# Attention heads of two sequences planned as couples: ten query blocks in five groups of scores, values placed beside a later group

## The chip, the core and the metric

The kernel runs on one core of one Trainium2 chip. Its engines are TensorE (PE; its weight loads are listed apart as PEld), VectorE (DVE), ScalarE (ACT), GpSimd (POOL) and SyncE (SP), which issues the DMAs. The metric is device time in microseconds (us) of one execution, the median of several runs. Every engine works its own list of instructions in order and waits on semaphores for the others.

## The reference, cut to what matters

```python
# x: (8, 512, 1024) float32; 16 heads of 64; everything in float32
def attention(h):                    # h = layernorm(x)
    q, k, v = h @ Wq, h @ Wk, h @ Wv           # split into 16 heads
    q, k = rotary(q), rotary(k)
    logits = einsum("bhqd,bhkd->bhqk", q, k)   # causal: -1e9 above the diagonal
    attn = softmax(logits / 8)
    return einsum("bhqk,bhkd->bhqd", attn, v) @ Wo
x = x + layernorm(attention(layernorm(x)))
x = x + layernorm(layernorm(x) @ W.T + bias + lora)
```

## The kernel before, in words

All large products are made by a two-level fast scheme: a product is cut into 7 x 7 = 49 small ones. One small product is a *tick*. Work that goes beside the products is planned by hand: `at(tick, fn, kind)` puts a function on a tick, and `run(tick, filler)` (L177) issues a tick in this order: first every event of kind `"pe"` (work for PE), in the order in which the events were planned; then the tick's small product with its drain (`filler`); then the plain events and the `"post"` events, again in the order of planning. Nothing reorders the instructions afterwards: this is each engine's list.

The kernel has four parts. First the values V of all eight sequences are computed and stored (`vd`). Then the QK loop makes queries and keys and runs the attention beside them. Then come the output projection and the feed-forward product, with the norms beside them.

The QK loop has `UQ` = 8 *stages* (`u`, L995 to L1010) of 49 ticks. A stage makes Q and K of eight heads for two sequences. `unit_product` (L953) issues its tick: four matmuls of 128x256, which the trace lists as eight records (L636), then the drain of the product before (L113 to L129: one or two copies or sums of 512 columns out of PSUM, on DVE or ACT), then the load of the slot eight ticks ahead (L608 to L622: 2 x 256 KB; the ring has nine slots). `plan_unit` (L691) puts the combining sums (L654) and the rotary embedding (`rotate`, L660 to L690) into a stage, mostly from tick 33 on to tick 14 of the next stage; the four rotations of a stage work on DVE and POOL with instructions of 1024 columns and end in DMAs (L687), eight for each, that spread Q and K into the tile `qk`. As `cq` has one buffer of each tag, a later drain into `A_q`, `B_q`, `D_q`, `E_q` or `F_q` must wait until the DMAs that read the tile have landed.

The attention of stage `u` - 1 runs in stage `u`. Its unit is a *pair*: two heads (j = 0, 1; 64 partitions each) of one sequence. A stage has `PAIRS` = 8 of them: four head tiles `i`, each for two sequences `s`. A pair has four query blocks of 128 rows; by causality block `qb` needs (qb + 1) x 128 key columns. The methods of `Pair` are:

- `load` (L735): the values of the pair, one DMA of 256 KB (pool `v`, three buffers).
- `scores` (L739): two matmuls per query block, one for each head, into a PSUM tile `s` of [128, 2, 512] floats, of which there is one buffer. The heads use partitions 0 to 63 and 64 to 127 of the operands.
- `exps` (L757): per block and head one DVE instruction (scale, mask, row minimum; L768) and one ACT exponential with its sum (L778), into a tile `pr` (four buffers).
- `scale` (L783): per block a reciprocal on DVE (L786) and two multiplications on ACT (L792).
- `transpose` (L794) and `keep` (L810): 128x128 transposes on PE into two PSUM tiles `tp` (two buffers) and copies into `pT`, by ACT for head 0 and by DVE for head 1.
- `values` (L823) and `store` (L835): eight matmuls of 512 to 128 columns with 64 output partitions per head, then one copy by DVE.
- `sum` (L847): four subtractions on POOL and two DMAs, for the last head tile only.

`Pair.plan` (L860) puts a pair on the ticks from `base`: scores of the groups (0, 1), (2,) and (3,) on +0, +2, +4 (384, 384 and 512 columns a head), their scaling on +4, +6, +8, their transposes on +6, +8, +10 (6, 6 and 8 blocks for the two heads), the values on +12. In stages 1 to 6 the pairs start 6 or 7 ticks apart (L1000 to L1002). So the values of one pair, the transposes of the next and the scores of the one after mostly fall on one tick. Stage 7 carries the pairs of stage 6 five ticks apart, and those of stage 7 follow behind with little beside them.

Of the kernel before, what the change touches and what calls it, by code (L numbers as in the profile page):

```python
# [10 lines left out]
F32 = mybir.dt.float32  # L11
I32 = mybir.dt.int32
AF = mybir.ActivationFunctionType
ALU = mybir.AluOpType
# [118 lines left out]
def sandwich_kernel(  # L133
# [587 lines left out]

    ops = {}

    class Pair:


        def __init__(self, u, n):
            self.u = u
            self.i, self.s = divmod(n, 2)
            self.g, bp = divmod(u, B // 2)  # L730
            self.b = 2 * bp + self.s
            self.name = f"{u}_{n}"
            self.pr, self.sm, self.ps = {}, {}, {}

        def load(self):  # L735
            self.v = work2["v"].tile([P, NT, P], F32, tag="v", name=f"v_{self.name}")
            nc.sync.dma_start(out=self.v, in_=vd[self.b][:, :, ts(NH * self.g + self.i, P)])

        def scores(self, qbs):  # L739
            qT, kT = (qk[self.u, self.i][:, :, self.s, w] for w in range(2))  # L740
            ps = ps_s.tile([P, 2, S], F32, tag="s", name=f"s_{self.name}_{qbs[0]}")
            at = 0
            for qb in qbs:
                L = (qb + 1) * P
                for j in range(2):
                    r = slice(j * HD, (j + 1) * HD)
                    nc.tensor.matmul(  # L747
                        ps[:, j, at : at + L],
                        lhsT=qT[r, qb],
                        rhs=kT[r, : qb + 1],  # L750
                        start=True,
                        stop=True,
                    )
                self.ps[qb] = ps[:, :, at : at + L]
                at += L

        def exps(self, qbs):  # L757
            pr = work2["work"].tile([P, 2, S], F32, tag="pr", bufs=4, name=f"pr_{self.name}_{qbs[0]}")
            at = 0
            for qb in qbs:  # L760
                L = (qb + 1) * P
                v = self.pr[qb] = pr[:, :, at : at + L]
                at += L
                nm = work2["small"].tile([P, 2], F32, tag="nm", name=f"nm_{self.name}_{qb}")
                sm = self.sm[qb] = work2["small"].tile([P, 2], F32, tag="sm", name=f"sm_{self.name}_{qb}")
                for j in range(2):

                    nc.vector.tensor_tensor_reduce(  # L768
                        out=v[:, j, :],
                        in0=self.ps[qb][:, j, :],  # L770
                        in1=work2["mask"][:, S - L :],
                        scale=-1.0 / HD**0.5,
                        scalar=3.0e38,
                        op0=ALU.add,
                        op1=ALU.min,
                        accum_out=nm[:, j : j + 1],
                    )
                    nc.scalar.activation(  # L778
                        v[:, j, :], v[:, j, :], AF.Exp,
                        bias=nm[:, j : j + 1], scale=-1.0, accum_out=sm[:, j : j + 1],  # L780
                    )

        def scale(self, qbs):  # L783
            for qb in qbs:
# [7 lines left out]
                        nc.scalar.mul(v, v, rs[:, j : j + 1])  # L792

        def transpose(self, qbs):  # L794
            if qbs[0] == 0:
                self.pT = [
                    work2["work"].tile([P, NT, S], F32, tag="pT", name=f"pT_{self.name}_{j}")
                    for j in range(2)
                ]
            self.pt = []  # L800
            for j in range(2):
                pt = ps_t.tile([P, NT, P], F32, tag="tp", name=f"ptp_{self.name}_{qbs[0]}_{j}")
                n = 0
                for qb in qbs:
                    for kb in range(qb + 1):
                        nc.tensor.transpose(pt[:, n, :], self.pr[qb][:, j, ts(kb, P)], ident)  # L806
                        n += 1
                self.pt.append(pt)

        def keep(self, qbs):  # L810
            for j in range(2):

                n = self.u * PAIRS + 2 * self.i + self.s - (UQ - 1) * PAIRS
                act = -2 <= n < 1 or j == 0 and (n < 0 or qbs[0] != 2)
                copy = nc.scalar.copy if act else nc.vector.tensor_copy
                if qbs[0] == 0:
                    copy(self.pT[j][:, 0, 0 : 2 * P], self.pt[j][:, 0:2, :])
                    copy(self.pT[j][:, 1, P : 2 * P], self.pt[j][:, 2, :])
                else:
                    (qb,) = qbs  # L820
                    copy(self.pT[j][:, : qb + 1, ts(qb, P)], self.pt[j][:, : qb + 1, :])  # L821

        def values(self):  # L823
            self.po = po = ps_v.tile([P, S], F32, tag="v", name=f"po_{self.name}")
# [35 lines left out]
        def plan(self, base, last=12, alone=False):  # L860

            A, B2, C3 = (0, 1), (2,), (3,)
            at(base - 4, self.load)
            for k, qbs in ((0, A), (2, B2), (4, C3)):
                at(base + k - alone, lambda qbs=qbs: self.scores(qbs), "pe")
                at(base + k - alone, lambda _, qbs=qbs: self.exps(qbs), "post")
            for k, qbs in ((6, A), (8, B2), (10, C3)):
                at(base + k - (4 if alone else 2), lambda qbs=qbs: self.scale(qbs))
                at(base + k, lambda qbs=qbs: self.transpose(qbs), "pe")
                at(base + k, lambda _, qbs=qbs: self.keep(qbs), "post")  # L870
            at(base + last, self.values, "pe")
            if alone:
                last += 2
                at(base + last, self.store)
            else:
                at(base + last, lambda _: self.store(), "post")
            if self.i == NH - 1:
                for m, k in enumerate((0, 0, 0, 0, 1) if alone else (1, 2, 3, 4, 6)):
                    at(base + last + k, lambda m=m: self.sum(m))

    products(-B, B, lambda q: ORDER)
    psum.close()
# [112 lines left out]
    for u in range(UQ + 1):  # L995
        base = u * N2
        if u < UQ:
            plan_unit(u, base)
        if 0 < u < UQ - 1:
            for n in range(PAIRS):  # L1000
                first = 10 if u > 1 else 12
                Pair(u - 1, n).plan(base + first + (n * (N2 + 10 - first) + PAIRS // 2) // PAIRS)  # L1002
        elif u == UQ - 1:
            for n in range(PAIRS):
                Pair(u - 1, n).plan(base + 9 + 5 * n, last=11)
            for n in range(PAIRS):
                Pair(u, n).plan(base + 51 + 6 * n, alone=True)
        if u < UQ:
            for n in range(base, base + N2):
                run(n, lambda n=n: unit_product(n))  # L1010
        else:
            run(base, lambda: cur.drain(NP))
            for k in range(base + 1, base + 10):
                run(k, None)
            streams.close()
            chunks.close()

            wop, gp, cl = (tc.alloc_tile_pool(name=name, bufs=1) for name in ("w2", "g2", "cl"))
            env["cl"] = cl
            tl = tc.alloc_tile_pool(name="tl", bufs=1)  # L1020
            for k, n in (
                (10, "R11"), (10, "L11"), (15, "R12"), (17, "R22"), (21, "L12"), (24, "R21"), (31, "L22"), (42, "S1"),
            ):
                if n in ("R11", "R12", "R21", "R22"):
                    at(base + k, lambda n=n: load_right(gp, 0, n))
                else:
                    at(base + k, lambda n=n: load_sums(wop, "wo", n, n))
            for k, n in ((21, "T1"), (26, "T2"), (32, "T4"), (44, "T3")):
                for m in range(3):
                    at(base + k + m, lambda n=n, m=m: sum_right(gp, 0, n, nc.gpsimd, slice(m, m + 1)))  # L1030
            at(base + 57, next_roles)
            for n in ("R12", "R11", "R21"):
                at(base + 57, lambda n=n: load_right(gp, 1, n))
            at(base + 52, lambda: combine(0, "c11", "c11", "A", nc.vector))
            cur, ticks = None, [*range(20, 44, 3), *range(44, 57)]
            for k in range(10, 57):
                if k in (51, 56):
                    n = {51: "S2", 56: "S4"}[k]
                    load_sums(wop2, "wo", n, n)
                if k == 49:  # L1040
                    rows_qk.close()
                    wop2 = tc.alloc_tile_pool(name="w2b", bufs=1)
                    load_sums(wop2, "wo", "S3", "S3")
                if k in ticks:
                    run(base + k, lambda n=ticks.index(k): first_product(n))
                else:
                    run(base + k, None)
            cur.drain(NP)
            run_rest()
# [311 lines left out]
```

## Time and profile before

| | |
|---|---|
| three timed runs, median (lowest to highest) | 2499.29 us (2498.07 to 2499.87) |
| profiled execution, its span | 2491.9 us |
| its time outside the span | not on the page; the median of the runs is 7.4 us above the span |
| mean granted TensorE clock | 0.988 |
| busy: PE, PEld, DVE, ACT, POOL | 2394.2, 1880.4, 1744.9, 1094.4, 1490.5 us |
| start of stages 2, 3, 4, 5, 6, 7 (first tick, in the timeline) | 657.2, 807.5, 956.1, 1105.1, 1253.8, 1402.6 us |

The page is one execution. A row of the timeline reads: start, length, engine, line of the kernel, operation, output<-inputs, shape, number of merged records, and in brackets the idle time before it with what ended it. PE's matmuls overlap in the pipeline and their ends are modelled, so the length of a row is not what it costs; the difference between its start and the start of the next row is. A window row reads: stretch, its length, then the busy time of each engine in it.

### The profile page before, as it was taken

What the parts mean: (1) busy time and instruction counts of PE and PEld (TensorE: products, weight loads), DVE (VectorE), ACT (ScalarE), POOL (GpSimd) and SP (SyncE); (2) the same over time, 40 slices, a digit from 0 to 9 for tenths busy, and PEclk for the clock granted to TensorE, in tenths of its full rate; (3) what the DMA queues carried; (4) which work ended last, traced back from release to release, by engine and by line L of the source; (5) the groups of instructions that cost most, each with busy time, mean ns of one, the idle gap of its engine ahead of it and who ended that gap; (6) DMA issues with size and microseconds to landing.
All of it is one profiled execution on the core that took longest, in us unless ns stands there. A gap on an engine that the chain in (4) does not pass through costs nothing. (4 is left out here: it accounts for less than half of the span.)

```text
span 2491.9 us, 37087 instructions
## 1 busy us (share of the span) xinstructions
PE 2394.2 (96%) x12192; PEld 1880.4 (75%) x12192; DVE 1744.9 (70%) x3849; ACT 1094.4 (44%) x2749; POOL 1490.5 (60%) x1119
## 2 busy tenths in 40 slices
PE   6999999999999999999999999899999999999997
PEld 4787887877677777777777776458888878888886
DVE  8777767475857759486775957766777777766676
ACT  3323331026555556555555565763444544222222
POOL 3878875215263454637465363426777687888885
PEclk8999999999999999999999999899999999999999
DMA  7697787999899898988989895657566676434334
GB/s 261 198 299 251 241 272 235 344 307 285 238 302 285 258 328 255 328 267 297 326 264 346 250 327 174 219 182 266 178 202 212 217 278 240 137 126 153 132 106 140
DMA packets 415665, 606.00 MB, mean 243 GB/s; under 512 B 127889, under 2 KB 243601, under 8 KB 410866
## 3 DMA queue, kind: packets, MB, share of 16 engines
q1 hardware_dynamic: 415474, 603.64, 73.9%
q8 instruction: 98, 1.61, 0.3%
q14 instruction: 93, 0.76, 0.1%
HBM read 368.65 MB, written 201.33 MB: 229 GB/s over the span
## 5 line engine op out<-in xcount | busy, mean ns | idle before, releaser
L778 ACT ACTIVATE pr<-pr,nm 128x128 f32<-128x128 f32 (+3 forms) x512 | 280.9, 550 | 169.7 <-DVE nm L768 169.6
L792 ACT ACTIVATE pr<-pr,rs 128x128 f32<-128x128 f32 (+2 forms) x500 | 245.2, 549 | 119.9 <-DVE rs L786 119.8
L768 DVE CUSTOM_DVE_ANT_0 pr<-s,mask 128x128 f32<-128x128 f32 (+3 forms) x512 | 224.1, 484 | 41.8 <-PE s L747 39.7
L636 PE MATMUL acca_q_P<-xs,ls 128*128 128x256 f32 x896 | 217.3, 385 | 0.8 <-issue 0.8
L636 PE MATMUL accc_q_P<-xs,ls 128*128 128x256 f32 x896 | 217.7, 386 | 0.0
L636 PE MATMUL accb_q_P<-xs,ls 128*128 128x256 f32 x896 | 216.3, 384 | 0.8 <-DVE u_q_P L116 0.8
L1107 POOL TENSOR_TENSOR c<-c,row 128x512 f32<-128x512 f32 x120 | 160.7, 1360 | 87.4 <-ACT c L415 80.3
L636 PEld LDWEIGHTS acca_q_P<-xs,ls 128*128 128x128 f32 x896 | 165.3, 190 | 49.9 <-issue 19.1
L636 PEld LDWEIGHTS accc_q_P<-xs,ls 128*128 128x128 f32 x896 | 165.8, 190 | 48.4 <-issue 23.2
L636 PEld LDWEIGHTS accb_q_P<-xs,ls 128*128 128x128 f32 x896 | 165.4, 190 | 44.9 <-issue 6.2
L275 POOL TENSOR_TENSOR T<-R,T 128x512 f32<-128x512 f32 (+1 forms) x96 | 174.1, 1840 | 41.4 <-DVE u_P L337 21.0
L747 PE MATMUL s<-qk 64*128 64x128 f32 (+3 forms) x1024 | 193.8, 474 | 5.1 <-DVE nm L768 4.7
L806 PE MATMUL ptp<-ident,pr 128*128 128x128 f32 x1280 | 178.7, 278 | 11.0 <-DVE nm L768 4.8
L806 PEld LDWEIGHTS ptp<-ident,pr 128*128 128x128 f32 x1280 | 147.7, 142 | 43.1 <-ACT pr L792 15.8
L827 PE MATMUL po<-pT,v 128*64 128x512 f32 (+3 forms) x1024 | 157.4, 446 | 9.7 <-ACT pT L821 9.7
L562 POOL TENSOR_TENSOR wc_g<-wc_g 128x256 f32<-128x256 f32 (+1 forms) x120 | 124.1, 1053 | 65.5 <-DMA wc_g<-in_wqk_dram 43.5
L678 POOL TENSOR_TENSOR B_q<-B_q,m 128x1024 f32<-128x1024 f32 x14 | 35.0, 2497 | 199.0 <-DVE B_q L675 199.0
L827 PEld LDWEIGHTS po<-pT,v 128*64 128x64 f32 x1024 | 72.4, 139 | 102.0 <-issue 66.5
L337 DVE TENSOR_TENSOR p_P<-accb_P,p_P 128x256 f32<-128x256 f32 x109 | 45.0, 413 | 102.4 <-PE accb_P L315 53.5
L636 PE MATMUL accd_q_P<-xs,ls 128*128 128x256 f32 x448 | 108.7, 385 | 0.0
L337 DVE TENSOR_TENSOR u_P<-accb_P,p_P 128x256 f32<-128x256 f32 x109 | 46.1, 423 | 89.1 <-ACT p_P L342 89.0
L747 PEld LDWEIGHTS s<-qk 64*128 64x128 f32 x1024 | 73.1, 187 | 46.2 <-issue 27.9
(1108 smaller groups left out, 5809.7 us busy)
## 6 DMA issues: line engine op xcount, KB each, us to landing
ls<-wqk SPq DMA_DIRECT2D x392, 256.0 KB, 4.9
xs<-xop SPq DMA_DIRECT2D x392, 256.0 KB, 5.2
R<-attn SPq DMA_DIRECT2D x32, 896.0 KB, 5.5
wqk<-wc_g SPq DMA_DIRECT2D x16, 1568.0 KB, 9.3
x<-in_x_dram SPq DMA_DIRECT2D x32, 512.0 KB, 9.5
v<-vd SPq DMA_DIRECT2D x64, 256.0 KB, 5.0
attn<-ops SPq DMA_DIRECT2D x16, 1024.0 KB, 7.8
row<-in_x_dram SPq DMA_DIRECT2D x32, 512.0 KB, 5.9
```

The lines of the kernel that those rows point to most:

```text
L275: eng.tensor_tensor(RX[q, n][:, c], RX[q, x][:, c], RX[q, y][:, c], op=ALU.subtract)
L337: add = lambda out, x, a: nc.vector.tensor_tensor(out, acc[a], x, op=ALU.add)
L562: eng.tensor_tensor(out, x, y, op=op)
L636: nc.tensor.matmul(acc[:, :, w, :], lhsT=ls[:, k, w, :], rhs=xs_[:, :, k, :], start=(first and w == 0 and k == 0), stop=True, skip_group_c ...
L678: eng.tensor_tensor(v, v, m[step - 4, q], op=ALU.add)
L747: nc.tensor.matmul(ps[:, j, at : at + L], lhsT=qT[r, qb], rhs=kT[r, : qb + 1], start=True, stop=True,)
L768: nc.vector.tensor_tensor_reduce(out=v[:, j, :], in0=self.ps[qb][:, j, :], in1=work2["mask"][:, S - L :], scale=-1.0 / HD**0.5, scalar=3.0e38,
L778: nc.scalar.activation(v[:, j, :], v[:, j, :], AF.Exp, bias=nm[:, j : j + 1], scale=-1.0, accum_out=sm[:, j : j + 1],)
L792: nc.scalar.mul(v, v, rs[:, j : j + 1])
L806: nc.tensor.transpose(pt[:, n, :], self.pr[qb][:, j, ts(kb, P)], ident)
L827: nc.tensor.matmul(po[j * HD : (j + 1) * HD, kb * P :], lhsT=self.v[:, kb, ts(j, HD)], rhs=self.pT[j][:, kb, kb * P :], start=(kb == 0), s ...
L1107: nc.gpsimd.tensor_tensor(c, c, row[q, t][:, ts(h, HALF)], op=ALU.add)
```

## The change

Two module-level helpers, `scores` and `exps`, take a list of (pair, query block), so that a group may hold blocks of two pairs. The methods of `Pair` call them. `keep` opens the tiles `pT` itself, and handles any list of blocks.

`plan_couple` is new. It plans the two sequences' pairs of one head tile, `a` and `b`, together: groups of scores a0+a2, a3, a1+b1, b0+b2, b3 (512 columns a head each) on ticks +0, +2, +5, +7, +10; transposes a(0, 2) on +6, a3 on +8, a1 on +10, b(0, 2) on +13, b1 on +14, b3 on +15 (8, 8, 4, 8, 4, 8 blocks for the two heads); the scaling of each group two ticks ahead of its transposes, except a1 and b3 (one tick) and b1 (five); the values of `a` on the start of the next couple, those of `b` five ticks later. Stages 1 to 6 plan four couples in place of eight pairs, 12 ticks apart (one step a stage is 13, in stage 1 it is 11). Stage 7 is planned as before.

```diff
+    def scores(parts):
+        p, qb = parts[0]
+        ps = ps_s.tile([P, 2, S], F32, tag="s", name=f"s_{p.name}_{qb}")
+        at = 0
+        for p, qb in parts:
+            qT, kT = (qk[p.u, p.i][:, :, p.s, w] for w in range(2))
+            L = (qb + 1) * P
+            for j in range(2):
+                r = slice(j * HD, (j + 1) * HD)
+                nc.tensor.matmul(
+                    ps[:, j, at : at + L], lhsT=qT[r, qb], rhs=kT[r, : qb + 1], start=True, stop=True
+                )
+            p.ps[qb] = ps[:, :, at : at + L]
+            at += L
+    def exps(parts):
+        p, qb = parts[0]
+        pr = work2["work"].tile([P, 2, S], F32, tag="pr", bufs=4, name=f"pr_{p.name}_{qb}")
+        at = 0
+        for p, qb in parts:
+            L = (qb + 1) * P
+            v = p.pr[qb] = pr[:, :, at : at + L]
+            at += L
...
         def scores(self, qbs):
...
+            scores([(self, qb) for qb in qbs])
         def exps(self, qbs):
...
+            exps([(self, qb) for qb in qbs])
...
         def transpose(self, qbs):
-            if qbs[0] == 0:
-                self.pT = [
-                    work2["work"].tile([P, NT, S], F32, tag="pT", name=f"pT_{self.name}_{j}")
-                    for j in range(2)
-                ]
...
         def keep(self, qbs):
+            if not self.pT:
+                self.pT = [
+                    work2["work"].tile([P, NT, S], F32, tag="pT", name=f"pT_{self.name}_{j}")
+                    for j in range(2)
+                ]
...
-                if qbs[0] == 0:
+                if qbs == (0, 1):
                     copy(self.pT[j][:, 0, 0 : 2 * P], self.pt[j][:, 0:2, :])
                     copy(self.pT[j][:, 1, P : 2 * P], self.pt[j][:, 2, :])
                 else:
-                    (qb,) = qbs
-                    copy(self.pT[j][:, : qb + 1, ts(qb, P)], self.pt[j][:, : qb + 1, :])
+                    n = 0
+                    for qb in qbs:
+                        copy(self.pT[j][:, : qb + 1, ts(qb, P)], self.pt[j][:, n : n + qb + 1, :])
+                        n += qb + 1
...
+    def plan_couple(u, i, base, after):
+        a, b = (Pair(u, 2 * i + s) for s in range(2))
+        for p in (a, b):
+            at(base - 4 + 5 * p.s, p.load)
+        for k, parts in (
+            (0, [(a, 0), (a, 2)]), (2, [(a, 3)]), (5, [(a, 1), (b, 1)]), (7, [(b, 0), (b, 2)]), (10, [(b, 3)]),
+        ):
+            at(base + k, lambda parts=parts: scores(parts), "pe")
+            at(base + k, lambda _, parts=parts: exps(parts), "post")
+        for k, m, p, qbs in (
+            (6, 4, a, (0, 2)), (8, 6, a, (3,)), (10, 9, a, (1,)),
+            (13, 11, b, (0, 2)), (14, 9, b, (1,)), (15, 14, b, (3,)),
+        ):
+            at(base + m, lambda p=p, qbs=qbs: p.scale(qbs))
+            at(base + k, lambda p=p, qbs=qbs: p.transpose(qbs), "pe")
+            at(base + k, lambda _, p=p, qbs=qbs: p.keep(qbs), "post")
+        for p, k in ((a, after), (b, after + 5)):
+            at(k, p.values, "pe")
+            at(k, lambda _, p=p: p.store(), "post")
+            if i == NH - 1:
+                for m, n in enumerate((1, 2, 3, 4, 6)):
+                    at(k + n, lambda p=p, m=m: p.sum(m))
...
         if 0 < u < UQ - 1:
-            for n in range(PAIRS):
-                first = 10 if u > 1 else 12
-                Pair(u - 1, n).plan(base + first + (n * (N2 + 10 - first) + PAIRS // 2) // PAIRS)
+            first = 10 if u > 1 else 12
+            starts_ = [base + first + (n * (N2 + 10 - first) + 2) // 4 for n in range(5)]
+            for n in range(NH):
+                plan_couple(u - 1, n, starts_[n], starts_[n + 1])
```

More of the change, by code (lines that the diff above doesn't have):

```diff
@@ L722, in sandwich_kernel @@
     ops = {}
+    def scores(parts):
[20 more added lines that the diff above has]
+            at += L
+            nm = work2["small"].tile([P, 2], F32, tag="nm", name=f"nm_{p.name}_{qb}")
+            sm = p.sm[qb] = work2["small"].tile([P, 2], F32, tag="sm", name=f"sm_{p.name}_{qb}")
+            for j in range(2):
+                nc.vector.tensor_tensor_reduce(
+                    out=v[:, j, :],
+                    in0=p.ps[qb][:, j, :],
+                    in1=work2["mask"][:, S - L :],
+                    scale=-1.0 / HD**0.5,
+                    scalar=3.0e38,
+                    op0=ALU.add,
+                    op1=ALU.min,
+                    accum_out=nm[:, j : j + 1],
+                )
+                nc.scalar.activation(
+                    v[:, j, :], v[:, j, :], AF.Exp,
+                    bias=nm[:, j : j + 1], scale=-1.0, accum_out=sm[:, j : j + 1],
+                )
     class Pair:
@@ L732, in __init__ @@
             self.name = f"{u}_{n}"
-            self.pr, self.sm, self.ps = {}, {}, {}
+            self.pr, self.sm, self.ps, self.pT = {}, {}, {}, None
         def load(self):
@@ L739, in scores @@
         def scores(self, qbs):
[L740 to L755, printed above, removed]
-        def exps(self, qbs):
[L758 to L781, printed above, removed]
+            scores([(self, qb) for qb in qbs])
+        def exps(self, qbs):
+            exps([(self, qb) for qb in qbs])
         def scale(self, qbs):
```

## The prediction

> **What bounds the kernel now.** Words first: a stage is one `u` of the QK loop, 49 ticks; a tick is one product (8 records of 128x256 at L636). S is a group of scores (L747), T a group of transposes (L806; T6 and T8 by the number of 128x128 blocks), V the values of a pair (L827). I read the page's shares, then the busy time by stage, then TensorE's (PE's) timeline, then that of VectorE (DVE).
>
> ```profile
> PE 2394.2 (96%) x12192; PEld 1880.4 (75%) x12192; DVE 1744.9 (70%) x3849; ACT 1094.4 (44%) x2749; POOL 1490.5 (60%) x1119
> ```
>
> The window of stage 4 (columns: stretch, its length, then busy us of PE, PEld, DVE, ACT, POOL, then clock, DMA share, GB/s):
>
> ```profile
> 956.00:1105.00 149.00, 148.91 (x810) 107.94 (x808) 106.14 (x258) 85.69 (x238) 81.98 (x56) 1.00 0.90 299
> ```
>
> PE is never idle there, so the stage lasts as long as PE's list. In the view of waits over the whole span, PE's waits at S, T and V are only 4.7, 10.8 and 9.7 us. What counts is what each piece takes from its start to the start of the next one, and that depends on the neighbour. PE's timeline in stage 4 (start, length, operation):
>
> ```profile
> 1052.38 1.13 PE L747 MATMUL s<-qk 64*128 64x512 f32 x4
> 1053.44 1.99 PE L636 MATMUL acca_q_P<-xs,ls 128*128 128x256 f32 x8
> 1055.27 1.89 PE L636 MATMUL accd_q_P<-xs,ls 128*128 128x256 f32 x8
> 1057.09 2.38 PE L827 MATMUL po<-pT,v 128*64 128x512 f32 x16
> 1059.40 0.87 PE L806 MATMUL ptp<-ident,pr 128*128 128x128 f32 x6
> 1060.11 1.89 PE L636 MATMUL accc_q_P<-xs,ls 128*128 128x256 f32 x8
> 1061.93 0.93 PE L747 MATMUL s<-qk 64*128 64x128 f32 x8
> 1062.79 1.99 PE L636 MATMUL acca_q_P<-xs,ls 128*128 128x256 f32 x8
> 1064.62 0.82 PE L806 MATMUL ptp<-ident,pr 128*128 128x128 f32 x6
> 1065.27 1.89 PE L636 MATMUL accb_q_P<-xs,ls 128*128 128x256 f32 x8
> ...
> 1069.77 1.04 PE L806 MATMUL ptp<-ident,pr 128*128 128x128 f32 x8
> 1070.64 1.89 PE L636 MATMUL accb_q_P<-xs,ls 128*128 128x256 f32 x8
> ```
>
> Differences of starts give the prices: S of 512 columns 1.06 us, S of 384 columns 0.86, V 2.31, T6 0.65 (0.05 more behind V), T8 0.87. A tick is 1.83 between S and T and 1.92 between S and V; between two T (the first output products behind stage 7, L977) it is 1.73. So a tick is 1.74, plus an **edge** of 0.09 behind S or V and of 0.09 ahead of S or V; T has no edge to a product. A T directly ahead of an S takes 0.09 more (at 1195.23: T6 0.75), which is the same edge. With these prices a stage of 49 ticks is 148.7 us; stages 3 to 6 last 148.6 to 149.0. The list explains the time.
>
> **The change, part by part.** No matmul, transpose, copy, exponential, reciprocal or DMA is added or removed; the built programs hold the same number on DVE and ACT. What changes is grouping and order, for 24 couples (4 each in stages 1 to 6).
>
> 1. *Scores.* Per couple, four S of 384 and two of 512 become five of 512: 4 x (0.86 + 0.18) + 2 x (1.06 + 0.18) = 6.64 against 5 x 1.24 = 6.20, so -0.44. The first two-block group (128 and 384) is not in the trace; the group of 128 and 256 costs what the single 384 costs (0.86 against 0.85), so I take 1.06, by that nearest row; the far end is 1.26 (the step from 384 to 512 paid once more), +14 us over the 72 groups of two blocks.
> 2. *Transposes.* Four T6 and two T8 (4 x 0.65 + 2 x 0.87 = 4.34) become four T8 and two T4. T4 is not shown: by the step T6 to T8 (0.22) it is 0.43, so 4.34 again: 0. Bounds 0.33 (half of T6) to 0.54 (T6 less half that step), 5 us to either side over 48 of them.
> 3. *Neighbours.* Before, V mostly stands ahead of T and its far edge becomes 0.05: 2.45 in all with the front edge. After, V stands directly ahead of S. One place of stage 7 shows that pair:
>
> ```profile
> 1450.21 2.37 PE L827 MATMUL po<-pT,v 128*64 128x512 f32 x16
> 1452.51 0.92 PE L747 MATMUL s<-qk 64*128 64x384 f32 x4
> 1453.36 1.99 PE L636 MATMUL accc_q_P<-xs,ls 128*128 128x256 f32 x8
> ```
>
> V takes 2.30 and S 0.85: no edge between them. Two pieces share their edges: V and S apart cost 2.49 + 1.24, together 3.55: -0.18, against -0.04 before; two per couple, -0.28. S directly ahead of T4 (once per couple) drops an edge, -0.09; no undisturbed row shows it, and the tail of the stage-7 heads, where waits mix in, has S of 512 ahead of T at 1.16 and T6 behind S at 0.99, so the bounds are 0 and +0.34, 8 us over all.
>
> Per couple -0.44 - 0.28 - 0.09 = -0.81; x 24 = -19.4. Counted instead over every tick of the two built orders, which catches the seams between stages: -2.8 (stage 1), -2.4, then -3.3 in each of stages 3 to 6, -0.9 in stage 7: **-19.2 us**.
>
> [...]
>
> 4. *New waits.* Two transposes per couple now come one tick after their `scale` (the first sequence's block 1, ticks +9 and +10; the second's block 3, +14 and +15); before, always two ticks. The reciprocal stands in DVE's queue, the scaling in ACT's. Where DVE is free this fits: reciprocal 0.15 and two scalings of 512 in 1.34 against a tick of 1.74 or more. But from tick 38 to about tick 6 of the next stage DVE has no gap at all, as the rotations and sums stand there:
>
> ```profile
> 1087.38 0.54 DVE L821 COPY pT<-ptp 128x384 f32<-128x384 f32 x1
> ...
> 1089.46 1.21 DVE L654 TENSOR_TENSOR D_q<-D_q,E_q 128x1024 f32<-128x1024 f32 x1
> 1090.60 1.21 DVE L654 TENSOR_TENSOR A_q<-A_q,D_q 128x1024 f32<-128x1024 f32 x1
> 1091.84 1.23 DVE L654 TENSOR_TENSOR D_q<-D_q,E_q 128x1024 f32<-128x1024 f32 x1
> ```
>
> In the changed order the third couple's block 1 is scaled at tick 44, behind two of these sums and the drain (0.69); the sum ahead of them took 3.06 (1084.40). Laid end to end, DVE reaches the reciprocals 3.3 us after tick 44 starts and ACT has scaled one head 0.6 and both 1.0 later; PE is at that T4 after 1.83 + 1.06 = 2.9. Wait: 1.2 us. Behind T4 on PE stand the tick's product and all that follows, so the end pays it. Bounds: 0 (if the 3.06 were 1.21) to 3. Block 3 at tick 50: 0.2. Five stages x 1.4 = +7.0. At the seam of stages 1 and 2 it stands one tick later, behind a 2.1 to 2.6 us sum, with a tick of only 0.43 + 1.74 to cover sum, copy 0.42, reciprocal 0.15 and scalings 1.4: +3.0 once (0 to 5).
>
> S on S: the smallest slack between the last read of the scores' PSUM tile (`s`, one buffer) and the next S was 1.3 us in stages 2 to 6 but for one place; the median is 3.0 and groups grow by 0.26 us. Nothing.
>
> 5. *Old waits.* In stage 1 DVE stood 7.17 us until the stores of the rotated tile landed, and PE with it:
>
> ```profile
> 560.07 0.69 DVE L116 TENSOR_TENSOR D_q<-accc_q_P,p_q_P 128x512 f32<-128x512 f32 x1 [7.17 <-DMA qk<-D_q]
> ```
>
> This landing stays where it is, so PE's ticks before it (which cost 0.8 more in the new order) do not matter: the sum from there on is -20.0. Behind it PE's timeline lost another 2.2; the new order has fewer copies there, so I take 0.5: -1.7. Around 645 to 671 us PE lost 3.7 over the prices; half goes: -1.9.
>
> Sum: -20.0 + 7.0 + 3.0 - 1.7 - 1.9 = **-13.6 us**. The span is 2491.9; the median of the three timed runs, 2499.29, is 7.4 more, taken as fixed. That gives a span of 2478.3 and a time of **2486**.
>
> **Rivals.**
> - *All of it arrives* (17%). DVE runs ahead at tick 44; only the seam waits: 2499.3 - 20 - 1 = 2478. For: PE's waits in stages 2 to 6 are near nothing now. Against: DVE's full stretch.
> - *The edges do not go* (16%): V-S keeps 0.18 (+8.3) and S-T4 costs up to 0.34 (+8). 2486 + 8.3 + 2 = 2496, at most 2502; two-block groups that cost more would end there too. For: the V-S row is one. It counts as no change.
> - *DMA takes the gain back* (4%). The share is 0.90, but a ring load lands in 5 us (page: 4.9 and 5.2) and is issued 8 ticks, some 24 us, ahead: 2495 to 2499.
> - *Slower: the one-tick scale* (9%). If the 48 transposes that come one tick after their scale wait on average more than 20/48 = 0.42 us, the gain is gone; over 0.52 the kernel is measurably slower. That is a queue of about one DVE sum of 1.2 us in front of the reciprocal everywhere, not only in the full stretch. With a mean of 0.8 the time is 2499 - 20 + 38 = 2517. Against: outside ticks 38 to 6 DVE is idle between groups, and the scaling needs 1.5 us of a tick.
>
> **Numbers.** Forecast 54%: 2486, by itself 2480 to 2493. All chances with it: 54 + 17 + 16 + 4 + 9. Range 2476 to 2500: it leaves out the slow rival and the tails of the first two. Faster by over 0.2% (under 2494.3): 54 + 17 + some 3 of the edges' case = 74%; within 0.2% (about what a measurement of this kernel can tell from no change) 17%; slower 9%.
>
> **What would show it.** 168 groups of scores for 192, those of 512 at 1.06; V to S without an edge; stages 3 to 6 at 146.5 to 147 us (by prices 145.4); PE waiting for ACT's scaling at T some 1 us near tick 45 of each stage; the 7 us wait for the stored tile in stage 1 still there. A stage window of 148 or more, or waits of T all over the stage, makes the prediction wrong.

## The result, and the profile after

The changed kernel takes 2519.89 us (median of four runs, 2515.99 to 2520.64), the kernel before 2499.58 beside it (four runs). The ratio is 1.0075, 95% interval 1.0057 to 1.0093: slower. Forecast were 2486 us and a range of 2476 to 2500. The profiled execution took 2520.64 us, its span is 2518.9 and its mean granted clock 0.984 (before 2491.9 and 0.988).

The page of the kernel after, its busy times:

```profile
PE 2393.8 (95%) x12192; PEld 1883.7 (75%) x12192; DVE 1742.3 (69%) x3849; ACT 1093.9 (43%) x2749; POOL 1488.4 (59%) x1119
```

All counts and nearly all busy times are those of before. So the 27 us between the two spans are time in which PE stands. Stage 4 as a window, after:

```profile
970.60:1121.20 150.60, 147.59 (x809) 107.76 (x808) 104.88 (x258) 85.65 (x238) 81.16 (x56) 1.00 0.89 295
```

Before, PE was busy for 148.91 us of 149.00; now it is busy for 147.59 and idle for 3.0. In stages 2 and 3 the stretch is longer still, 157.9 and 156.5 us. The view of waits for PE from 656 to 1400 us (after: stage 2 to most of stage 6) names what it stands for (columns: who waited for what; us in total, times, the longest). After:

```profile
PE s L734 <- DMA qk<-D_q: 12.3, 7, 4.7
PE ptp L807 <- ACT pr L798: 6.0, 5, 2.4
```

Before, the same view of 656 to 1400 us holds one line, of 0.6 us:

```profile
PE ptp L806 <- ACT pr L792: 0.6, 2, 0.4
```

The second line of after was forecast (the scaling one tick ahead). The first was not: scores wait for a DMA that brings queries and keys. PE's timeline in stage 3, tick 10, after:

```profile
842.32 2.38 PE L835 MATMUL po<-pT,v 128*64 128x512 f32 x16
844.62 0.49 PE L734 MATMUL s<-qk 64*128 64x128 f32 x4
849.84 2.58 PE L734 MATMUL s<-qk 64*128 64x384 f32 x4 [4.72 <-DMA qk<-D_q]
852.35 3.78 PE L636 MATMUL accb_q_P<-xs,ls 128*128 128x256 f32 x8
```

This is the first group of the first couple, a0+a2. Block 0 (128 columns) runs at once behind V; block 2 (384 columns) stands 4.72 us, and then it and the product behind it are slow as well: 2.51 and 3.57 us from start to start in place of 0.86 and 1.83 (the granted clock is 0.50 there, see the last section). The issues of SP at the same place say why, after:

```profile
841.53 0.61 SPq L553 DMA_DIRECT2D wc_g<-in_wqk_dram  x1
842.24 0.59 SPq L687 DMA_DIRECT2D qk<-E_q  x1
842.93 0.55 SPq L687 DMA_DIRECT2D qk<-D_q  x1
843.53 0.58 SPq L687 DMA_DIRECT2D qk<-E_q  x1
844.16 0.70 SPq L687 DMA_DIRECT2D qk<-D_q  x1
```

A query and key tile comes in two halves: blocks 0 and 1 from `B_q` and `F_q` (j = 0), blocks 2 and 3 from `E_q` and `D_q` (j = 1). Eight DMAs of such halves go out on tick 9, some 0.6 us apart. By the loop around L687 the first four, shown here, fill the second half of this head tile, two for each of its heads; the other four fill the next tile's, and block 2 does not read them. Ahead of them stands the load of a 512 KB weight chunk (`wc_g`). How long the fourth takes from its issue to its landing is in the view of L687 for that DMA alone (844.2:844.8), after:

```profile
DMA to landing us min/median/max: 6.5/6.5/6.5
```

So it lands at some 850.7, and block 2 on tick 10, which is reached at 845.1, asks for it more than 5 us too early: head 0 starts at 849.84, when its two DMAs are there, and head 1 behind the fourth. In the kernel before, the first group on tick 10 was blocks 0 and 1, of the first half; block 2 came on tick 12. That stood in its trace all along. The fourth DMA before, in SP's timeline and in the same view (836.95:837.6):

```profile
836.94 0.71 SPq L687 DMA_DIRECT2D qk<-D_q  x1
DMA to landing us min/median/max: 6.1/6.1/6.1
```

and PE before:

```profile
843.37 0.92 PE L747 MATMUL s<-qk 64*128 64x384 f32 x4
```

It lands at 843.0: 4.8 us after the group of tick 10 (838.21, blocks 0 and 1) has begun, and only some 0.3 us ahead of the group of tick 12 (843.37, block 2), which waits for nothing. Of the 5.2 us between the two ticks block 2 needed nearly all, and the change took them. In stage 2 the slack was the same; in stages 4 to 6, where no chunk load stands ahead of these DMAs, the fourth landed 3.2 to 3.9 us before its reader, so two ticks less cost less there.

The whole balance is in the table: for each stage the time over the prices of the prediction (starts of PE's pieces, less their prices; T4 behind S is counted at the 0.49 us that the rows show), from the profiled executions. "Both" is the run with the other first group and earlier scalings, "last" the one that adds swapped transposes, scalings two ticks behind the exponentials and earlier chunk loads (all below).

| stage | 1 | 2 | 3 | 4 | 5 | 6 | 7 | sum | prices |
|---|---|---|---|---|---|---|---|---|---|
| before | 8.4 | 1.6 | -0.1 | 0.3 | 0.0 | 0.1 | 2.8 | 12.9 | 1011.9 |
| after | 10.8 | 11.4 | 10.9 | 5.0 | 5.7 | 7.7 | 4.7 | 56.3 | 993.9 |
| both | 11.7 | 2.8 | 0.8 | 3.6 | 3.1 | 1.9 | 3.9 | 27.9 | 993.9 |
| last | 10.5 | 1.8 | 1.0 | 2.3 | 8.3 | 1.9 | 3.8 | 29.7 | 993.9 |

By prices the change saves 18.0 us, by waits and slow pieces it loses 43.4; with 0.8 of a later first group in stage 1 that is the 26 us by which the QK loop ends later. The 43.4 are: scores at tick 10 and what follows them in stages 2 to 6 (granted clock 0.50 in stages 2, 3 and 6, 1.00 in 4 and 5), 24.6; the transposes of ticks 45 and 46 in these stages, 10.0; transposes waiting for the buffers of `tp` at tick 12, 3.2; ticks 36 and 37 (the other scaling of one tick), 2.0; stage 1, 2.4; stage 7, 2.0; the rest are small ones of either sign.

### The profile page after: what moved, and what is told of

Same layout as the page of the kernel before. It is cut to its first block, busy times and chain, and to the rows that moved or that the text cites. A ratio compares the mean times of both kernels' runs of the same rounds, so it can differ in the third digit from the quotient of the medians.

```text
span 2518.9 us, 36983 instructions
## 1 busy us (share of the span) xinstructions
PE 2393.8 (95%) x12192; PEld 1883.7 (75%) x12192; DVE 1742.3 (69%) x3849; ACT 1093.9 (43%) x2749; POOL 1488.4 (59%) x1119
## 5 line engine op out<-in xcount | busy, mean ns | idle before, releaser
L636 PE MATMUL accb_q_P<-xs,ls 128*128 128x256 f32 x896 | 223.1, 393 | 1.2 <-DVE u_q_P L116 0.8
L835 PE MATMUL po<-pT,v 128*64 128x384 f32 (+3 forms) x1024 | 157.3, 448 | 12.0 <-ACT pT L828 12.0
L678 POOL TENSOR_TENSOR B_q<-B_q,m 128x1024 f32<-128x1024 f32 x14 | 35.0, 2497 | 199.0 <-DVE B_q L675 199.0
L828 DVE COPY pT<-ptp 128x128 f32<-128x128 f32 (+2 forms) x225 | 108.3, 502 | 43.3 <-PE ptp L807 28.5
L828 ACT COPY pT<-ptp 128x128 f32<-128x128 f32 (+2 forms) x223 | 91.5, 435 | 52.5 <-PE ptp L807 30.7
```

The costliest lines, as they stand in the source:

```text
L636: nc.tensor.matmul(acc[:, :, w, :], lhsT=ls[:, k, w, :], rhs=xs_[:, :, k, :], start=(first and w == 0 and k == 0), stop=True, skip_group_c ...
L828: copy(self.pT[j][:, : qb + 1, ts(qb, P)], self.pt[j][:, n : n + qb + 1, :])
L835: nc.tensor.matmul(po[j * HD : (j + 1) * HD, kb * P :], lhsT=self.v[:, kb, ts(j, HD)], rhs=self.pT[j][:, kb, kb * P :], start=(kb == 0), s ...
```

## The experiments

The theory, L: the change moves block 2 of the first couple to a tick at which its half of `qk` has not yet landed, and that is most of the loss; the late scalings are a second, smaller part. The rivals: the order of the groups itself is what costs, with whatever it reads (R); or VectorE as a whole is behind, and time won at one tick is lost at the next (D). Each kernel's median stands beside that of before on the same chip: 2496.6 us for the kernel with the other first group, the old one with block 2 first, the one with the chunk load out of the way and the one with earlier scalings, 2496.7 for the other six. After was measured beside a before of 2499.6, so a gain on after is given twice where they differ: by the medians, and by the ratios (their difference x 2497 us).

**Another first group.** The first couple begins with the blocks of the first half; its scalings and transposes follow that order, and nothing else is touched.

```diff
+        ) if i else (
+            (0, [(a, 1), (b, 1)]), (2, [(a, 0), (a, 2)]), (5, [(a, 3)]), (7, [(b, 0), (b, 2)]), (10, [(b, 3)]),
...
+        ) if i else (
+            (6, 4, a, (1,)), (8, 6, a, (0, 2)), (10, 9, a, (3,)),
+            (13, 11, b, (0, 2)), (14, 9, b, (1,)), (15, 14, b, (3,)),
```

> The changed kernel (2519.9 us), but the first couple of each stage begins with the group a1+b1, which reads only key and query blocks 0 and 1; a0+a2 follows two ticks later and a3 three ticks after that. Theory L (landing): the scores of block 2 at the couple's first tick read the second half of the rotated tile, whose eight DMAs go out only one tick earlier; in stages 2 to 6 that costs 8.1 + 8.7 + 2.7 + 2.4 + 3.8 = 25.6 us with what waits behind, and in stage 1 most of the 7 us there comes back as the old wait for the stored tile. So 2494 (2488 to 2499), and no wait for a DMA ahead of the scores at tick 10. Rival D (late scaling: the transposes that come one tick after their scale hold PE everywhere): 2515 or more. Rival P (the prices of the pieces were wrong, groups of 512 or the V-S neighbours cost more than thought): 2515 or more.

Measured 2503.34 us, ratio 1.0024 [1.0013, 1.0034]. The direction is right, 16.6 us off after's time (12.7 by the ratios); the size is not: 2494 was expected. PE has no wait for `qk` left in stages 2 to 6, and stages 2 and 3 fall to 3.4 and 2.4 us over the prices. But stages 4 to 6 rise, to 7.1, 8.6 and 7.2. What was won there was given back at ticks 40 to 45; the run with the chunk loads below shows to whom.

**The kernel before, with block 2 first.** The sufficiency of L: the old pairs, but the first pair of a stage takes block 2 on its first tick and blocks 0 and 1 two ticks later (stages 1 to 6).

```diff
-            for k, qbs in ((0, A), (2, B2), (4, C3)):
+            for k, qbs in ((0, B2 if swap else A), (2, A if swap else B2), (4, C3)):
```

> The kernel before (2499.3 us), but in stages 1 to 6 the first pair takes its group of block 2 on its first tick and the group of blocks 0 and 1 two ticks later (transposes exchanged likewise). Nothing else is changed. Theory L: this alone brings the wait for the landing of the second half, 2 to 3 us in stages 4 to 6 and 6 to 8 in stages 2 and 3 : 2519 (2512 to 2526). Rivals D and P: no change, 2499.

Measured 2512.18 us, ratio 1.0058 [1.0042, 1.0075]: at the lower end of what L gave, far from the rivals. One moved group of one pair per stage makes the old kernel 15.6 us slower (14.5 by the ratio). PE's timeline of this run, stage 3:

```profile
848.83 2.40 PE L747 MATMUL s<-qk 64*128 64x384 f32 x4 [4.19 <-DMA qk<-D_q]
851.16 3.78 PE L636 MATMUL accb_q_P<-xs,ls 128*128 128x256 f32 x8
```

It is the picture of after: the same kind of wait (4.19), and slow pieces behind it (lengths 2.40 and 3.78, after 2.58 and 3.78). Stages 2 and 3 now stand 7.6 and 8.0 us over the prices (before 1.6 and -0.1), stages 4 to 6 only 1.2 to 1.4.

**The chunk load out of the way.** After, with the chunk load of stages 2 and 3 on tick 5 and no longer on tick 9, ahead of the DMAs of `qk`.

```diff
-        ... if u == 1 else (9, 19, 29):
+        ... if u == 1 else (5, 19, 29) if u in (2, 3) else (9, 19, 29):
```

> The changed kernel, but in stages 2 and 3 the load of a 512 KB weight chunk, planned on tick 9 just ahead of the eight DMAs of the rotated tile, moves to tick 5 (its sums and its store move with it). In the changed kernel the last of the eight waits 2.1 us for that load to land, in stages 2 and 3 only. Theory L: the waits of stages 2 and 3 shrink from 8.4 to about 2.5 us each: 2508 (2505 to 2514). Rivals D and P: 2520.

Measured 2507.09 us, ratio 1.0034 [1.0021, 1.0047], as expected (12.8 us below after, 10.2 by the ratios). Tick 10 of stages 2 and 3 now stands 1.9 us over the prices, about as in stages 4 to 6, where after had 8.1 and 8.4; so the chunk load made three quarters of it there. The rest is four DMAs 0.6 us apart and a landing. The view of L687 for the four DMAs of stage 3, after (842.2:844.8) and in this run (832.0:834.5), has the landing twice as fast without the load ahead:

```profile
DMA to landing us min/median/max: 6.5/6.7/7.1
DMA to landing us min/median/max: 3.0/3.1/3.3
```

PE in stage 3 of this run, where each head waits for its own two DMAs:

```profile
836.00 0.88 PE L734 MATMUL s<-qk 64*128 64x384 f32 x2 [0.45 <-DMA qk<-D_q]
837.22 0.88 PE L734 MATMUL s<-qk 64*128 64x384 f32 x2 [0.34 <-DMA qk<-D_q]
```

The product behind these short waits costs 1.83 us from start to start (838.03 to 839.86): no half pace.

**The same order, other data.** After, order and ticks and all, but block 2 of the first couple reads data of the half that is there.

```diff
+                n, k = qb, kT[r, : qb + 1]
+                if p.i == 0 and qb == 2:
+                    n, k = 1, kT[r, :1].broadcast_to([HD, 3, P])
```

> After as it is, order and ticks and all, but the first couple's group of block 2 reads its query from block 1 and its keys from block 0 three times over, so the scores of block 2 of these two sequences' heads are computed from other data, of the half that is there early; the outputs of that block of that couple are other numbers. The same count and shape of products. Theory L (the wait for the landing of the second half of the query and key tile, some 33 us in stages 1 to 6, of which stage 1 keeps its 7 at the next group): 2520 - 25 = 2495, or 2495 to 2505 when a part is given back later in the stage as in the run with the other first group (2503). Rival R (the order of groups itself, the full groups' eviction or the products next to each other cost the time, not the data that is read): 2516 to 2521, as after.

Measured 2504.41 us, ratio 1.0028 [1.0018, 1.0038]: 15.5 us below after (11.7 by the ratios), so R falls: the order is the same, and without the landing it costs that much less. As with the other first group, a part is given back in stages 4 to 6 (5.3, 7.9, 7.3 over the prices). The group at that place in stage 3, PE of this run:

```profile
835.98 1.14 PE L737 MATMUL s<-qk 64*128 64x128 f32 x8
837.05 1.99 PE L636 MATMUL accb_q_P<-xs,ls 128*128 128x256 f32 x8
```

This is the price of the prediction: a group of 128 and 384 columns 1.07, from its start to that of the product; V ahead of it has 2.30 again.

**Earlier scalings.** After, with the two scalings that stood one tick ahead of their transposes put two ticks ahead.

```diff
-            (6, 4, a, (0, 2)), (8, 6, a, (3,)), (10, 9, a, (1,)),
-            (13, 11, b, (0, 2)), (14, 9, b, (1,)), (15, 14, b, (3,)),
+            (6, 4, a, (0, 2)), (8, 6, a, (3,)), (10, 8, a, (1,)),
+            (13, 11, b, (0, 2)), (14, 9, b, (1,)), (15, 13, b, (3,)),
```

> The changed kernel, but block 1 of the first sequence is scaled on tick +8 in place of +9 and block 3 of the second on +13 in place of +14: two ticks ahead of their transposes, as before the change. Theory L: only the waits at the third couple's block 1 (ticks 45 or 46 of stages 1 to 6; 10.5 us in the trace) go, most of them: 2512 (2508 to 2516). Rival D: this is the main loss, 2490 to 2500. Rival P: 2520.

Measured 2512.94 us, ratio 1.006 [1.0045, 1.0075]: 7.0 us less than after by the medians, as expected, but 3.7 by the ratios, whose intervals overlap; what is certain is the place in the trace. That place in stage 5, tick 45, PE after:

```profile
1257.08 1.13 PE L734 MATMUL s<-qk 64*128 64x512 f32 x4
1260.58 0.84 PE L807 MATMUL ptp<-ident,pr 128*128 128x128 f32 x4 [2.37 <-ACT pr L798]
```

and in this run:

```profile
1253.68 1.13 PE L734 MATMUL s<-qk 64*128 64x512 f32 x4
1254.74 0.66 PE L807 MATMUL ptp<-ident,pr 128*128 128x128 f32 x4
1255.23 1.89 PE L636 MATMUL accb_q_P<-xs,ls 128*128 128x256 f32 x8
```

S to T4 is 1.06 us, T4 to the product 0.49: prices again, once the wait is out of the way.

**Both edits.** The other first group and the earlier scalings together (the scores as in the run with the other first group).

```diff
...
             (6, 4, a, (0, 2)), (8, 6, a, (3,)), (10, 8, a, (1,)),
             (13, 11, b, (0, 2)), (14, 9, b, (1,)), (15, 13, b, (3,)),
+        ) if i else (
+            (6, 4, a, (1,)), (8, 6, a, (0, 2)), (10, 8, a, (3,)),
+            (13, 11, b, (0, 2)), (14, 9, b, (1,)), (15, 13, b, (3,)),
```

> After with both earlier edits at once: the first couple's first group takes block 1 of both sequences in place of blocks 0 and 2 of one (2503 us alone, 16.6 below after), and the scalings of a's and b's last groups go out one tick earlier (2513 alone, 7 below after). If the landing of the second half of query and key and the late scalings are two separate causes (theory L), the two gains add: 2519.9 - 16.6 - 7 = 2496 (2492 to 2500), about the time of before, and the T4 piece at tick 45 starts within 0.3 us in stages 2 to 6. If the waits in stages 4 to 6 are those of a VectorE that is behind as a whole (theory D: what is given back at one tick is lost at the next), the scaling's tick is worth nothing once the landing is gone: 2501 to 2505, with the waits moved to other ticks of the same stages.

Measured 2491.98 us, ratio 0.9982 [0.9973, 0.9991]. The two gains add, to more than their sum (27.9 us against 16.6 and 7.0; by the ratios 23.2 against 12.7 and 3.7), and D falls: at 2501 to 2505 it would have been. With both causes away the change is a gain, if a small one.

**The second sequence's transposes swapped**, on top of both edits, in all couples.

```diff
-            (13, 11, b, (0, 2)), (14, 9, b, (1,)), (15, 13, b, (3,)),
+            (13, 9, b, (1,)), (14, 11, b, (0, 2)), (15, 13, b, (3,)),
```

> The run before this one (first group and scales) with one more edit: the second sequence's block 1 is transposed at tick 13 of its couple and its blocks 0 and 2 at tick 14, instead of the other way round, which puts the four-block transposes one tick farther behind the previous couple's evictions and their two buffers. Theory L counts the wait for these buffers at tick 12 of a stage at 0.6 to 1 us in stages 2 to 6, so 3 to 4 us below that run: 2492 (2488 to 2496). Theory D: nothing, within 2 us of that run.

Measured 2497.84 us, ratio 1.0000 [0.9991, 1.0010]: a miss for both theories, 5.9 us worse than without it. The wait at tick 12 that it was to remove is still there (0.6 to 1.1 us in each stage): whichever transposes stand on that tick find their `tp` buffer not yet emptied by VectorE. The profile puts most of the rest into stage 6 (4.5 us at ticks 28, 40 and 41) and 2 us into stage 1; why there, one profile does not settle.

**Every scaling two ticks behind its exponentials**, on top of that.

```diff
+            (6, 2, a, (0, 2)), (8, 4, a, (3,)), (10, 7, a, (1,)),
+            (13, 7, b, (1,)), (14, 9, b, (0, 2)), (15, 12, b, (3,)),
+        ) if i else (
+            (6, 2, a, (1,)), (8, 4, a, (0, 2)), (10, 7, a, (3,)),
+            (13, 2, b, (1,)), (14, 9, b, (0, 2)), (15, 12, b, (3,)),
```

> The run before this one (swapped transposes) with every scaling put two ticks behind its group's exponentials, which is 1 to 7 ticks earlier than it was; nothing else is moved. If a late reciprocal on VectorE is what the transposes of stages 4 to 6 wait for (late scaling), a further 2 to 5 us go: 2488 (2485 to 2492). If it is VectorE's whole work that is late (theory D), the reciprocals merely push the evictions and the reductions back: within 2 us of that run or slower.

Measured 2489.22 us, ratio 0.9971 [0.9960, 0.9982]: in the range that L gave, but 8.6 us better than the run before, where 2 to 5 were expected. No transpose of stages 2 to 6 waits for a scaling any more.

**Earlier chunk loads, with the other first group alone.** What takes time back in stages 4 to 6? VectorE and GpSimd there, in the run with the other first group:

```profile
1214.10 5.34 POOL L562 TENSOR_TENSOR wc_wf<-wc_wf 128x256 f32<-128x256 f32 x6 [7.51 <-DMA wc_wf<-in_wf_dram]
...
1219.38 4.66 POOL L654 TENSOR_TENSOR F_q<-F_q,E_q 128x1024 f32<-128x1024 f32 x2
...
1221.77 3.35 DVE L672 TENSOR_TENSOR m<-F_q,sin 128x1024 f32<-128x1024 f32 x1 [3.73 <-POOL F_q L654]
...
1243.30 1.12 PE L807 MATMUL ptp<-ident,pr 128*128 128x128 f32 x4 [2.42 <-ACT pr L798]
```

GpSimd waits until its chunk has landed, sums it (5.34), and only then adds into `F_q`; VectorE's rotation waits 3.73 us for that sum, and everything in VectorE's queue behind it is late, down to the reciprocal of tick 44 and the transposes that need it, which wait 2.42 us. In after GpSimd waited 7.30 us for the same chunk and summed it in 5.34 (at 1231.33), and VectorE's rotation waited 1.11 (at 1239.02): GpSimd's part is nearly the same, and VectorE stood longer in the run whose PE had been faster. The edit, which is not of the change, moves the later loads of stages 4 to 6 ahead.

```diff
-        ... else (4, 13, 22, 31) if u in (4, 5, 6) ...
+        ... else (4, 12, 20, 28) if u in (4, 5, 6) ...
```

> The earlier run with the other first group (2503 us, where the landing wait is gone and stages 4 to 6 wait 23 us in all at ticks 12, 40, 41 and 45), with one more edit that is not of the change: in stages 4 to 6 the chunk loads of ticks 13, 22 and 31 go out at 12, 20 and 28, so that GpSimd's sums of the last chunk are done before its addition into F at tick 36, which VectorE's rotation of tick 38 reads. Theory P (what the saved time is given back to in stages 4 to 6 is GpSimd's last chunk: F is late, VectorE waits 3.7 us for it and then reaches everything up to the reciprocals of tick 44 late): the waits at 40 and 41 go and those at 45 fall to the 1.1 to 1.3 of stages 2 and 3, about 8 to 13 us: 2493 (2489 to 2496). Theory D (the scalings one tick ahead are late by themselves in stages 4 to 6): 2500 to 2504.

Measured 2496.55 us, ratio 0.9995 [0.9982, 1.0007]: 6.8 us below the 2503.34 without it, under the 8 to 13 expected but far from D's. The same place in this run:

```profile
1218.85 3.36 DVE L672 TENSOR_TENSOR m<-F_q,sin 128x1024 f32<-128x1024 f32 x1 [0.23 <-POOL F_q L654]
...
1239.93 0.84 PE L807 MATMUL ptp<-ident,pr 128*128 128x128 f32 x4 [1.01 <-ACT pr L798]
```

The waits of ticks 40 and 41 are gone, that of tick 45 is 1.0 in place of 2.4. In their place stands one at tick 28: 1.4 to 1.9 us in each of stages 4 to 6.

**Earlier chunk loads, with the scalings two ticks behind the exponentials.** The edit is the same line, in that kernel.

> The run with every scaling two ticks behind its exponentials (2489 us) with the same move of the chunk loads in stages 4 to 6 (12, 20, 28 in place of 13, 22, 31). Theory P: the waits at ticks 41 and 45 of stages 4 to 6, some 2.5 us a stage in that run, go for the larger part: 2484 (2480 to 2487). Theory D: 2487 to 2491, as without the move.

Measured 2488.89 us, ratio 0.9962 [0.9947, 0.9977]. The time is that of the run without the move (2489.22): the 5 us expected did not come. In the profiles ticks 45 and 46 of stages 4 to 6 fall from 2.0 to 2.3 us over the prices to 0 to 0.5. A wait at tick 28 of stage 5 stands in both; with the slow piece behind it (without the move a product of 3.51 us, at a clock of 0.50; with it scores of 2.01) it costs 4.5 us without the move and 6.2 with it. Where the gain went in the median is not shown: the profiled execution without the move was 7.4 us above its median. GpSimd, SP and VectorE in the timeline of this run:

```profile
1165.05 1.27 POOL L863 TENSOR_TENSOR opt<-ops 128x512 f32<-128x512 f32 x1 [11.10 <-DMA attn<-opt]
...
1180.76 0.37 SPq L865 DMA_DIRECT2D attn<-ops  x1
...
1188.07 0.69 DVE L850 COPY ops<-po 128x512 f32<-128x512 f32 x1 [8.47 <-DMA attn<-ops]
```

and a line of SP's waits from 1160 to 1192 us:

```profile
SPq L553 <- DMA wo_d<-wc_wo: 4.3, 1, 4.3
```

The output's sums of the second sequence wait until those of the first are stored (`opt` has one buffer). The last of them ends at 1174.5, but SP issues their store only at 1180.76: the load of the next chunk, which this edit moved, stands ahead of it and waits 4.3 us until the chunk's own store has landed. Without the move the store goes out 1.4 us behind its sums (at 1177.83). VectorE's copy into the two buffers of `ops` waits 8.47 us for the store's landing, and the row minima of that tick stand behind the copy; PE's next scores wait 3.43 us for them. GpSimd's wait is in the kernel before as well (5 times there, 54.5 us in all), where PE has no wait at tick 28. A second buffer of `opt` was not tried.

## Why the prediction was wrong

- **Prices: right.** -19.2 us were forecast; -18.0 is what the built order gives for the seven stages with T4 behind S at 0.49 in place of the 0.43 assumed. The rows bear the others out: V to S 2.30 without an edge (844.62 - 842.32 in after, where all 46 such boundaries of stages 1 to 7 take 2.30 or 2.31; 2.30 in the run with other data), S of 512 in two blocks 1.07, S ahead of T 1.06. The bounds for two-block groups and S to T4 held at their favourable end. The rival "The edges do not go" was no cause: its +8.3 is 0.18 for each of the 46 boundaries, and no run shows that term; they stood without an edge.
- **Old waits: wrong, and the place where the main miss could have been seen.** The prediction's fifth step looked at one landing, that of stage 1 ("This landing stays where it is"), because it had a wait in the trace of before. It did not ask of each moved group what it reads. In stage 1, too, the group a0+a2 meets that landing, at tick 12, where before only a drain met it at tick 18; the forecast of -3.6 us for the old waits became +2.4 in stage 1. (Of the 3.7 us that the prediction read at 645 to 671 us, the same prices give 2.9.)
- **New waits: a term is missing, the main step that failed.** The fourth step lists the scaling of one tick and puts everything else at nothing. Block 2 of the first couple went from tick 12 to tick 10 of stages 2 to 6; its slack was in the trace of before: in stage 3 the DMA that it reads landed 0.3 us ahead of it. That term cost 24.6 us in the profile of after; removing it alone gave 16.6 us (other first group) and 15.5 (other data), by the ratios 12.7 and 11.7, because stages 4 to 6 gave a part back.
- **The scaling: right in place and mechanism, near in size.** Forecast 1.2 us at tick 45 and 0.2 at tick 50 in five stages, and 3.0 at the seam, +10.0 in all. Ticks 45 and 46 of stages 1 to 6 cost 12.3 us, of which 1.01 to 2.37 in each of stages 2 to 6 is the wait itself; ticks 36 and 37, where the view names no wait, cost 2.0 more, and tick 12 cost 3.2. Taking away both scalings of one tick gave 7.0 us by the medians, 3.7 by the ratios.
- **"S on S: nothing": right.** From 656 to 1400 us of after no group waits for the scores' buffer.
- **The slower rival** had 2517 us, near the time measured, but by the one-tick scaling; that is worth 4 to 7 us of some 20. The number was near by accident.
- **The base.** The span was taken to be 7.4 us short of the median for all executions. In the executions recorded here the time is 1.7 to 3.1 us above the span, in the profiled ones with both on record 1.7 to 1.9; so the profiled execution of before was some 5 us faster than its median, and part of the 27 us between the spans is that.
- **What was not foreseen at all** is who stands next in line. With the landing and the scalings away 18 us of cheaper pieces give 4.7 us (2491.98 against 2496.7), and with the further edits 7.8: PE's list was shorter than the chains beside it allow. For GpSimd's chunk a run shows it (6.8 us with the other first group alone); for the output's store it is read from profiles, and no run changes it. Stage 3, where both edits leave 0.8 us of waits, lasts 146.4 us in that run, against 148.6 before and 146.5 to 147 forecast.

The cause of the loss is shown from three sides: undone in the order, undone in the data, and done alone to the old kernel. What stays open is the 5.9 us of the swapped transposes, where the gain of the last run went, and how much of its wait at tick 28 comes from GpSimd's wait for `opt` and how much from the chunk load ahead of the store.

## What to carry to other kernels

When a group of work is regrouped or moved to an earlier tick, list for each operand from which DMA or instruction it comes and when that lands in the trace of before, also where nothing waits for it today: a wait of zero with 0.3 us of slack, or with 3, is not a wait of zero two ticks (5 us) earlier. Count to the landing and not to the issue: the same DMA landed 3.1 us after its issue here, or 6.5 behind a large load. A tile that is filled in halves has two times of arrival; put the work that reads the first half first. And where one engine is busy for all of a stage, its saving can be bounded by the chains that just keep up with it (18 us of cheaper pieces gave 4.7 here, with both causes away): measure their slack before counting the saving in full.

## What the hardware showed that was not expected

**A pause of PE was paid twice in several places.** After a wait of 4.72 us in stage 3 PE ran at half clock. Windows of after (columns: stretch, length, busy us of PE, PEld, DVE, ACT, POOL, granted clock, DMA share, GB/s):

```profile
851.00:856.00 5.00, 5.00 (x12) 3.10 (x12) 1.47 (x8) 2.07 (x8) 0.00 (x0) 0.50 0.29 102
```

From about 849.5 to 856 the clock is 0.50. The pieces there take some 3.6 us more than their prices, on top of the 4.72 of the wait: S 2.51 for 0.86 (a part of it is head 1's wait for its own DMAs), the product 1.74 over its price, the transposes 0.2. In stage 5 of the run with the other first group a wait of 2.42 us was enough, and the clock was back after 3 us:

```profile
1244.00:1245.00 1.00, 1.00 (x4) 0.88 (x4) 1.00 (x5) 0.98 (x3) 0.00 (x0) 0.50 1.04 242
```

In stage 6 of after one of 1.64 us was enough (at 1412.25):

```profile
1414.00:1416.00 2.00, 2.00 (x6) 1.64 (x5) 0.34 (x2) 1.20 (x5) 0.00 (x0) 0.50 0.83 193
```

But after a wait of 2.37 us in stage 5 of after (at 1260.58) the clock stayed at 1.00, so the length of a single wait did not decide it alone:

```profile
1261.00:1262.00 1.00, 1.00 (x7) 0.92 (x7) 1.00 (x4) 0.97 (x3) 0.00 (x0) 1.00 0.97 225
```

Nor did a long one need to come first: in stage 6 of after it was 0.50 from 1307 to 1310, behind two waits of 0.32 and 0.48 (at 1303.94 and 1305.30). What else decides it, no run here shows.

**VectorE beside GpSimd.** A product of 1024 columns took 1.20 us on VectorE while GpSimd was idle (L672 at 1228.35 in the run with the other first group) and 3.35 and 3.36 beside GpSimd's additions into `F_q` (the two rows at L672 above). So the late chunk on GpSimd reached VectorE twice in that run: as a wait of 3.73 us, and as slower work.
